# A cross-attention block on one core: the last two pairs of batches in another order, with the last probabilities turned through DRAM

## The chip, the cores and the metric

The kernel runs on one core of one Trainium2 chip. The metric is the device time of one execution in microseconds (us); lower is better. The kernel before and the changed kernel compute the same function in 32-bit floating point throughout.

## The reference

The inputs are x and a context, both [128 batches, 128 positions, 256], and the weights of one layer: four 256x256 projections, a 256x1024 W1, a 1024x256 W2, biases, and two sets of norm factors. There are 16 heads of 16. With mask = 0 position i attends only to positions below i, and row 0 of the probabilities is set to zero:

```python
q = (query @ Wq + bq).reshape(b, s, N_HEADS, D_K).transpose(0, 2, 1, 3)
k = (key @ Wk + bk).reshape(b, s, N_HEADS, D_K).transpose(0, 2, 1, 3)
v = (values @ Wv + bv).reshape(b, s, N_HEADS, D_K).transpose(0, 2, 1, 3)
scores = jnp.einsum('bhqd,bhkd->bhqk', q, k) / jnp.sqrt(jnp.float32(D_K))
allowed = j < i + mask
scores = jnp.where(allowed, scores, NEG_INF)
attn = jax.nn.softmax(scores, axis=-1)
if mask == 0:
    attn = attn.at[:, :, 0, :].set(0.0)
ctx = jnp.einsum('bhqk,bhkd->bhqd', attn, v).transpose(0, 2, 1, 3).reshape(b, s, d)
x = layer_norm(query + ctx @ Wo + bo, ln1_g, ln1_b)
ffn = jax.nn.relu(x @ W1 + b1) @ W2 + b2
out = layer_norm(x + ffn, ln2_g, ln2_b)
```

Key and values are both the context.

## The kernel before, in words

Two batches make a pair; there are 64 pairs, 0 to 63, and NP is 64. The work is a software pipeline over pairs: while one pair's scores are made, earlier pairs are in their feed-forward part. The order on each engine is written out by hand (a manual schedule): each engine executes its instructions in the order of the program, and waits by itself where an operand or a buffer isn't there yet. That holds for the DMAs too: SP (and ACT, where ACT issues them) waits in its own order, and what is queued behind a waiting DMA waits with it.

One pair p goes through these steps, each a function of the kernel:

- queries, keys and values: projections on TensorE (eight 256-wide matmuls each), copied out by ACT.
- `scores_both`: the scores of the lower and upper halves of the rows ("low" has 64 columns a head, "high" 128). `mask`, `mask_high`, `low_maximum` on VectorE; `exponential_by_head` on ACT, one instruction for each head (L840); `reciprocal` on VectorE and `sums` on GpSimd (L444), which multiplies 1024 columns by the reciprocal sums.
- `turn` (L463): VectorE transposes 32x32 blocks of the probabilities into the tile tb, in three thirds (two high, one low). `bring` (L478): sixteen DMAs move strip i, block j of tb to strip j, block i of the tile pT, SBUF to SBUF, 96 KB each. Together the two make the full transpose.
- `weigh` (L510, L520; the tile pc): probabilities times values. `context` copies to cxT. `attention_out` (po): the product with Wo, eight 256-wide matmuls. `attention_sum`, `both_stats`, `both_shifts`, `norm1`: residual and first norm, by VectorE, GpSimd and ACT; x1 is the result.
- `turn_x1`: VectorE transposes x1 into tbx; `across` sends it to DRAM in four DMAs (x1t, L246) and fetches it in one (x1T, L249).
- `combine_normed` (xS) and `Hidden`: the product with W1, in seven block products in place of eight; each is eight matmuls of 128 columns (L989). `run(1, 6)` runs products 1 and 6; `keep` (ACT, L999) copies product 1 out of its bank of PSUM, and `u2`, `u3`, `add2` to `add5` (VectorE) add the others up in hT. Product 3 accumulates on product 5's bank, after `add5` has read it. `again` takes bank 2 a second time, for product 5, once `keep` has emptied it. `relus` (L1020) follows on ACT.
- `combine_hidden` (hS, four GpSimd instructions) and `Second`: the product with W2, again in seven block products (L893; tiles pX, py, pz), added to the residual t2 by `add` (L928).
- `residual1` (GpSimd) makes the residual with its biases; `norm2` and `finish` (or `norm2_apart` and `finish_apart`, in a bank of PSUM with VectorE) the second norm; `store` (L684) writes the output.

PSUM has eight banks, and each product names the bank it takes. `step(p)` for p = 7 to 62 runs, in this order on TensorE: weigh(p-2), scores(p), the projections, attention_out(p-2), the W2 products of pair p-4, the W1 products of pair p-3. At its end SP issues, in order, the x1t sends and x1T fetch of pair p-2, the store of pair p-5 and the sixteen pT DMAs of pair p.

After the loop stands the ending, for p = 63, where no projections of a further pair are left. On TensorE: weigh(61), scores(63), attention_out(61), values(63), all seven W2 products of pair 59, weigh(62), six W1 products of pair 60, and so on to the W2 products of pair 62. Of pair 63's pT DMAs SP issues eight and ACT eight, after all three turns. The very last W2 product (pair 63) is done in two halves of 16 plain 256-wide matmuls (py_last, L1671); each half is added to t2 (L1675), gets its statistics (L1677, L1678), its epsilon on VectorE (L1679), its power of -0.5 on GpSimd (L1680), and two multiplications with the factors of the norm (L680, L681) before its store (L1684).

## Time and profile before

| what | value |
|---|---|
| median of 3 runs | 1505.72 us (1505.43 to 1507.54) |
| the profiled execution | 1507.01 us |
| its span in the trace | 1505.2 us |
| mean granted clock of TensorE | 0.994 |
| TensorE, ACT, GpSimd, VectorE busy | 98%, 88%, 87%, 85% |
| DMA, mean of the span | 136 GB/s |

The span is the time from the first to the last recorded instruction; the profiled execution takes 1.8 us more. Busy shares are means over the whole span, so they say little of the last 90 us, which this change is about. A row of the trace in order of time gives start, duration, engine, line of the code, operation, tiles (out<-in), how many instructions are merged in it, and in brackets the idle time ahead of it with what ended it. PE is TensorE, DVE VectorE, POOL GpSimd, SPq and ACTq the DMAs that SP and ACT issue.

### The profile page before, as it was taken

The numbers are of one execution on the slowest core, as the hardware profiler recorded it, in microseconds if no ns is written. First come the engines' busy times: TensorE is split into PE (matmuls) and PEld (weight loads), VectorE is DVE, ScalarE is ACT, GpSimd is POOL, SyncE is SP. The second block draws the span as 40 slices with busy tenths as digits, with TensorE's granted clock in tenths as the row PEclk, the third lists the DMA queues.
The fourth block names the chain that finished last, engine by engine and source line by source line (L and its number), as shares of the span: only waits on it lengthen the run. The fifth ranks groups of instructions, "written<-read, shape, count | busy, mean of one in ns | idle before, by whom it ended". The sixth has DMA issues, their size and how long they took to land.

```text
span 1505.2 us, 54159 instructions
## 1 busy us (share of the span) xinstructions
PE 1481.1 (98%) x19366; PEld 1383.7 (92%) x19366; DVE 1282.0 (85%) x2735; ACT 1319.3 (88%) x5277; POOL 1304.5 (87%) x1308
## 2 busy tenths in 40 slices
PE   8999999999999999999999999999999999999888
PEld 7788999999999999999999999999999999999887
DVE  7989888888888898898898888898898888888846
ACT  5667999999999999999999999999999999999843
POOL 6878888988988988988988988988988989889956
PEclk9999999999999999999999999999999999999989
DMA  8356656566656566656566666566666566664431
GB/s 198 85 116 140 151 141 132 141 144 134 157 132 142 138 144 136 153 139 140 134 145 141 151 141 138 137 141 142 149 141 141 134 143 141 150 139 114 124 78 50
DMA packets 415321, 204.66 MB, mean 136 GB/s; under 512 B 282448, under 2 KB 383056, under 8 KB 415056
## 3 DMA queue, kind: packets, MB, share of 16 engines
q1 hardware_dynamic: 412768, 199.34, 57.2%
q8 instruction: 159, 2.61, 0.8%
q10 hardware_dynamic: 2288, 1.85, 0.5%
q14 instruction: 106, 0.87, 0.2%
HBM read 70.26 MB, written 33.29 MB: 69 GB/s over the span
## 4 chain that ended last, share of the span: by engine, by line
PE 91%; DVE 3%; DMA 2%; ACT 1%; POOL 1%; SPq 1%; issue 1%; POOLq 0%; DVEq 0%; ACTq 0%
PE phs L989 25%; PE pX L893 10%; PE pq L268 8%; PE py L893 7%; PE pv L308 7%; PE pz L893 7%; PE po L539 7%; PE pk L268 7%; PE pss L391 6%; PE pc L520 4%; PE pc L510 2%; PE ph L777 1%; SPq L478 1%; DMA pT<-tb 1%; ACT sm L840 0%
## 5 line engine op out<-in xcount | busy, mean ns | idle before, releaser
L444 POOL TENSOR_TENSOR sm<-sm,rs 128x1024 f32<-128x1024 f32 x192 | 361.8, 1899 | 11.6 <-PE phs L989 7.8
L840 ACT ACTIVATE sm<-pss,nmx 128x128 f32<-128x128 f32 x944 | 328.5, 404 | 37.9 <-issue 33.6
L840 ACT ACTIVATE sm<-sm,nmx 128x64 f32<-128x64 f32 x944 | 313.8, 405 | 0.0
L463 DVE STREAM_TRANSPOSE tb<-sm 128x1024 f32<-128x1024 f32 x186 | 226.2, 1219 | 32.7 <-POOL sm L444 32.7
L840 ACT ACTIVATION_READ_ACCUMULATOR sm<-sm,nmx 128x1 f32 x912 | 235.4, 258 | 0.0
L1020 ACT ACTIVATE hT<-hT,b1e_c 128x256 f32<-128x256 f32 x480 | 204.4, 499 | 27.9 <-DVE hT L1011 27.9
L840 ACT ACTIVATION_READ_ACCUMULATOR sm<-pss,nmx 128x1 f32 x912 | 222.5, 244 | 0.0
L989 PE MATMUL phs<-xS,w1t 128*128 128x128 f32 x1440 | 172.2, 276 | 5.2 <-ACT hT L999 5.2
L989 PEld LDWEIGHTS phs<-xS,w1t 128*128 128x128 f32 x1440 | 167.0, 193 | 5.4 <-ACT hT L999 5.4
L862 POOL TENSOR_TENSOR hS<-hT 128x512 f32<-128x512 f32 x60 | 76.1, 1269 | 91.2 <-ACT hT L1020 90.2
L823 DVE TENSOR_REDUCE nmx<-pss 128x4 f32<-128x512 f32 x236 | 150.8, 680 | 0.0
L298 ACT ACTIVATE kT<-pk,bkh,half 128x256 f32<-128x256 f32 x252 | 130.6, 588 | 4.0 <-PE pk L268 4.0
L989 PE MATMUL phs<-x1T,w 128*128 128x128 f32 x960 | 127.4, 276 | 0.6 <-DMA x1T<-x1t 0.6
L893 PE MATMUL pX<-wt,hS 128*128 128x128 f32 x960 | 126.8, 275 | 0.0
L268 PE MATMUL pq<-xT,wq 128*128 128x256 f32 x504 | 125.4, 392 | 0.0
L539 PE MATMUL po<-wo,cxT 128*128 128x256 f32 x512 | 121.3, 380 | 0.8 <-ACT cxT L532 0.8
L308 PE MATMUL pv<-wv,cT 128*128 128x256 f32 x512 | 120.9, 379 | 0.0
L268 PE MATMUL pk<-cT,wk 128*128 128x256 f32 x504 | 119.2, 379 | 0.0
L989 PEld LDWEIGHTS phs<-x1T,w 128*128 128x128 f32 x960 | 117.5, 193 | 0.9 <-PE pX L893 0.7
L893 PEld LDWEIGHTS pX<-wt,hS 128*128 128x128 f32 x960 | 116.8, 192 | 0.0
L405 DVE TENSOR_TENSOR sm<-pss,neg 128x256 f32<-128x256 f32 (+1 forms) x276 | 108.2, 435 | 7.3 <-PE pss L363 2.5
L539 PEld LDWEIGHTS po<-wo,cxT 128*128 128x128 f32 x512 | 96.8, 190 | 14.6 <-ACT cxT L532 1.3
(167 smaller groups left out, 3915.9 us busy)
## 6 DMA issues: line engine op xcount, KB each, us to landing
pT<-tb SPq DMA_DIRECT2D x976, 96.0 KB, 2.2
x1t<-tbx SPq DMA_DIRECT2D x252, 64.0 KB, 3.0
x1T<-x1t SPq DMA_DIRECT2D x63, 256.0 KB, 3.0
out_dram<-t SPq DMA_DIRECT2D x63, 256.0 KB, 3.2
xb<-in_x_dram SPq DMA_DIRECT2D x124, 128.0 KB, 4.2
cb<-in_ctx_dram SPq DMA_DIRECT2D x124, 128.0 KB, 3.8
x<-in_x_dram SPq DMA_DIRECT2D x31, 512.0 KB, 4.6
w<-in_L_xattn_W_dram SPq DMA_DIRECT2D x2, 1024.0 KB, 7.7
```

What stands on the lines that cost most here:

```text
L268: nc.tensor.matmul(ps[:, m * TP : (m + 1) * TP], w[:, k, m * P : (m + 1) * P], src[:, k, :], start=(k == 0), stop=(k == KC - 1),)
L298: nc.scalar.activation(st["kT"][:, m, e, :], pk[:, m * TP : (m + 1) * TP], AF.Identity, bias=bkh[:, m, e : e + 1], scale=half[:, e : e + 1],)
L308: nc.tensor.matmul(pv[:, s * D : (s + 1) * D], st["cT"][:, k, s * P : (s + 1) * P], wv[:, k, :], start=(k == 0), stop=(k == KC - 1),)
L405: nc.vector.tensor_tensor(st["sm", hi][:, 4 * r : 4 * r + 4, :], st["sps", hi][r][:, : 4 * n].rearrange("p (n j) -> p n j", j=n), no[:, No ...
L444: nc.gpsimd.tensor_tensor(sm[:, part, :], sm[:, part, :], rs[:, :, None].to_broadcast([P, part.stop - part.start, n]), ALU.mult,)
L463: nc.vector.transpose(st["tb"][:, :, at : at + 256].rearrange("p j (n a) -> p n j a", a=32), st["sm", hi].rearrange("p h j -> p (h j)")[:, ...
L539: nc.tensor.matmul(po[:, s * D : (s + 1) * D], cxT[:, k, s, :], wo[:, k, :], start=(k == 0), stop=(k == KC - 1),)
L823: nc.vector.tensor_reduce(st["nmx", 1][:, 4 * r : 4 * r + 4], st["sps", 1][r].rearrange("p (n j) -> p n j", j=P), AX.X, ALU.max, negate=True,)
L840: nc.scalar.activation(sm[:, h, :], src, AF.Exp, bias=nmx[:, h : h + 1], scale=1.0, **({"accum_out": st["su", hi][:, h : h + 1]} if summed ...
L893: nc.tensor.matmul(out, left(k), right(k), start=(first and k == 0), stop=(k == K - 1), skip_group_check=True,)
L989: nc.tensor.matmul(ps[:, i * P : (i + 1) * P].rearrange("p (n a) -> p n a", a=32), left(i), right, start=(i == 0 and which not in self.ONT ...
L1020: nc.scalar.activation(self.hT[:, f], self.hT[:, f], AF.Relu, bias=b1e_c[:, f : f + 1], scale=1.0,)
```

## The change

Nothing is changed before step 62, and no product is added or removed. What is reordered or replaced:

- **Step 62**: four of the sixteen pT DMAs of pair 62 are issued before the fetch of x1T(60), twelve after it, and the store of pair 57 last.
- **`turn_x1` is split** into `send_x1` and `fetch_x1`, which the ending calls apart.
- **pair 63's probabilities**: `send` writes a third of tb (512 KB) to DRAM in one DMA as soon as that third is turned; `fetch` reads it back transposed in four DMAs of 128 KB. All are issued by SP; ACT issues none.
- **order of the ending**: pair 59's first W2 product comes before attention_out(61); six W1 products of pair 60 come before weigh(62), values(63) after it; the low exponentials are cut into 4, 4 and 8 with norm1(61) and keep in between; the W2 products of pairs 60 to 62 start before product 3 of the next pair's W1, and weigh(63) stands among those of pair 60. `Hidden` is given its own bank for product 5 in each pair, so that `again` isn't called there. Norms, residuals and stores are moved to fit, and pair 60's last two VectorE operations are called apart.
- **last tile**: the sum with t2, the statistics and the first multiplication stay in PSUM; epsilon is added by GpSimd; the first multiplication of the first half comes before `finish_apart(62)`.

The diff up to the ending:

```diff
                 )
         return pt
-    def across(dst, src, name, queue):
+    def out_across(src, name, queue):
         n = src.shape[2]
...
             queue.dma_start(
                 mid[i].rearrange("j b n -> b j n"), src[32 * i : 32 * i + 32]
             )
+        return mid
+    def back(dst, mid, queue):
         queue.dma_start(dst, mid.rearrange("i j b n -> (j b) i n"))
     def tokens(p, which):
...
                 "p (n j a) -> p n j a", j=NS, a=32
             ),
         )
+    def send(p, t):
+        st = states[p]
+        if "pT" not in st:
+            pT = st["pT whole"] = wide(f"pT_{p}").rearrange("p (i n) -> p i n", i=NS)
+            st["pT"] = pT.rearrange("p i (n a) -> p i n a", a=32)
+        at = slice(256 * t, 256 * t + 256)
+        mid = st["through", t] = dram.tile([NS, 32, NS, 256], F32, tag=f"pTt{t}", name=f"pTt{t}_{p}", bufs=1)
+        nc.sync.dma_start(mid.rearrange("i b j n -> (i b) j n"), st["tb"][:, :, at])
+    def fetch(p, t):
+        st = states[p]
+        mid = st.pop(("through", t))
+        for j in range(NS):
+            nc.sync.dma_start(
+                st["pT whole"][32 * j : 32 * j + 32, :, 256 * t : 256 * t + 256],
+                mid[:, :, j].rearrange("i b n -> b i n"),
+            )
     def bring(p, queue, which):
...
                 ps[:, s], t2[:, s], AF.Identity, bias=nb[:, s], scale=sd[:, s]
             )
-    def finish_apart(p):
+    def finish_apart(p, parts=(0, 1)):
         t2, ps = states[p]["t2"], states[p]["pb"]
-        nc.vector.tensor_tensor(ps, ps, g2_r[:, None, :].to_broadcast([P, 2, D]), ALU.mult)
-        nc.vector.tensor_tensor(t2, ps, be2_r[:, None, :].to_broadcast([P, 2, D]), ALU.add)
-        store(p)
-    def norm_alone(t2, mean, sd):
-        nc.vector.scalar_tensor_tensor(t2, t2, mean, g2_r, ALU.subtract, ALU.mult)
-        nc.vector.scalar_tensor_tensor(t2, t2, sd, be2_r, ALU.mult, ALU.add)
+        if 0 in parts:
+            nc.vector.tensor_tensor(ps, ps, g2_r[:, None, :].to_broadcast([P, 2, D]), ALU.mult)
+        if 1 in parts:
+            nc.vector.tensor_tensor(t2, ps, be2_r[:, None, :].to_broadcast([P, 2, D]), ALU.add)
+            store(p)
     def store(p):
         nc.sync.dma_start(
...
-    def turn_x1(p, queue=nc.sync):
+    def turn_x1(p):
+        send_x1(p)
+        fetch_x1(p)
+    def send_x1(p):
         st = states[p]
         tb = ffn.tile([P, NS, 4 * 32], F32, tag="tbx", name=f"tbx_{p}", bufs=1)
         nc.vector.transpose(
             tb.rearrange("p j (u a) -> p u j a", a=32),
             st["x1"].rearrange("p s (k j a) -> p (s k) j a", k=KC, a=32),
         )
+        st["mid"] = out_across(tb, f"x1t_{p}", nc.sync)
+    def fetch_x1(p):
+        st = states[p]
         x1T = ffn.tile([P, NS, 4 * 32], F32, tag="x1T", name=f"x1T_{p}")
-        across(x1T, tb, f"x1t_{p}", queue)
+        back(x1T, st.pop("mid"), nc.sync)
         st["x1T"] = x1T.rearrange("p i (s k a) -> p s i k a", s=2, k=KC)
     def turn_x1_on_pe(p):
...
         def __init__(self, p, banks=None):
             st = states[p]
-            self.WHERE = banks or self.WHERE
+            if banks:
+                self.WHERE, self.AGAIN = banks, {}
             self.p, self.x1T, self.xs = p, st["x1T"], st["xS"]
             self.hT = st["hT"] = ffn.tile([P, FC, TP], F32, tag="hT", name=f"hT_{p}", bufs=2)
             self.h = self.hT.rearrange("p (i e) (s t) -> p e s i t", e=2, s=2)
...
         norm2(p - 5)
         h.add4()
         h.relus((0, 2, 4, 6))
-        turn_x1(p - 2)
+        send_x1(p - 2)
+        if p < NP - 2:
+            fetch_x1(p - 2)
         h.add3()
         turn(p, 0, 0)
         states[p - 3]["rest"] = h
...
         residual1(p - 3)
         hidden_by_seven(p)
         finish(p - 5)
-        store(p - 5)
-        bring(p, nc.sync, LATE_FIRST)
+        if p < NP - 2:
+            store(p - 5)
+            bring(p, nc.sync, LATE_FIRST)
+        else:
+            bring(p, nc.sync, LATE_FIRST[:4])
+            fetch_x1(p - 2)
+            bring(p, nc.sync, LATE_FIRST[4:])
+            store(p - 5)
     third()
     fourth()
```

The calls of the ending (p = 63) after the change, in their order, several to a line; h and w are the current objects of `Hidden` (W1) and `Second` (W2):

```python
weigh(p - 2); context(p - 2); states[p - 4]["rest"].relus((1, 7, 3, 5)); scores_both(p); add_bo(p - 1)
combine_hidden(p - 4, POOL_ALONE); combine_normed(p - 3); mask(p, 0, B); mask(p, 0, A); mask_high(p, A)
exponential_by_head(p, 1, ONES, True); w = Second(p - 4, banks=(4, 7, 6)); w.run(1); attention_out(p - 2)
attention_sum(p - 2); w.run(2, 4, 5); w.add(0); mask_high(p, B); exponential_by_head(p, 1, TWOS, True)
w.add(1); joint = both_stats((p - 2,), ()); both_shifts(*joint); residual1(p - 3); w.run(6); w.add(2)
low_maximum(p); exponential_by_head(p, 0, ONES[:4], True); norm1(p - 2)
exponential_by_head(p, 0, ONES[4:], True); reciprocal(p, 1, ONE); reciprocal(p, 1, TWO); sums(p, 1, ONE)
sums(p, 1, TWO); w.run(3); w.add(4, 3); w.run(7); w.add(5); add_bo(p)
h = Hidden(p - 3, {1: 2, 2: 6, 6: 5, 7: 3, 5: 0, 4: 1}); h.run(1, 2, 6); h.keep()
exponential_by_head(p, 0, TWOS, True); send_x1(p - 2); h.u2(); h.run(7, 5); h.u3(); turn(p, 1, 0); send(p, 0)
fetch_x1(p - 2); reciprocal(p, 0, ALL); h.add5(); turn(p, 1, 1); send(p, 1); fetch(p, 0); h.run(4); h.add2()
weigh(p - 1); context(p - 1); values(p); h.run(3); h.add4(); h.relus((0, 2, 4, 6)); h.add3()
h.relus((1, 7, 3, 5)); sums(p, 0, ALL); turn(p, 0, 0); send(p, 2); fetch(p, 1); fetch(p, 2); values_out(p)
attention_out(p - 1); combine_normed(p - 2); attention_sum(p - 1); joint = both_stats((p - 1,), ())
both_shifts(*joint); later = both_stats((), (p - 5, p - 4))
h = Hidden(p - 2, {1: 2, 2: 6, 6: 5, 7: 3, 5: 0, 4: 7}); h.run(1, 2, 6); h.keep(); norm1(p - 1)
combine_hidden(p - 3, POOL_ALONE); residual1(p - 2); both_shifts(*later); h.u2(); h.run(7, 5); h.u3()
send_x1(p - 1); fetch_x1(p - 1); h.add5(); h.run(4); h.add2(); h.add4(); h.relus((0, 2, 4, 6))
w = Second(p - 3, banks=(1, 6, 4)); w.run(1, 2); h.run(3); h.add3(); w.run(4); w.add(0); w.run(6); w.add(2)
w.run(5); weigh(p); context(p); w.run(7); residual1(p - 1); combine_normed(p - 1); h.relus((1, 7, 3, 5))
norm2(p - 5); norm2(p - 4); attention_out(p); w.add(1); attention_sum(p); joint = both_stats((p,), ())
both_shifts(*joint); w.run(3); w.add(5, 3, 4); joint = both_stats((), (p - 3,)); both_shifts(*joint)
combine_hidden(p - 2, POOL_ALONE); h = Hidden(p - 1, {1: 2, 2: 0, 6: 3, 7: 7, 5: 5, 4: 6}); h.run(1, 2, 6)
h.keep(); norm1(p); h.u2(); h.run(7, 5); h.u3(); send_x1(p); fetch_x1(p); h.add5(); h.run(4); h.add2()
h.add4(); norm2_apart(p - 3, 4); h.relus((0, 2, 4, 6)); w = Second(p - 2, banks=(1, 2, 0)); w.run(1); h.run(3)
h.add3(); h.relus((1, 7, 3, 5)); w.run(2, 4, 5); w.add(0, 3, 1); w.run(6); w.add(2); finish(p - 5)
store(p - 5); finish_apart(p - 3, (0,)); w.run(3); w.add(4); finish_apart(p - 3, (1,)); w.run(7); w.add(5)
combine_normed(p); combine_hidden(p - 1, POOL_ALONE); joint = both_stats((), (p - 2,)); both_shifts(*joint)
residual1(p); finish(p - 4); store(p - 4); h = Hidden(p, {1: 4, 2: 3, 6: 7, 7: 5, 5: 6, 4: 1})
h.run(1, 2, 4, 6); h.keep(); h.u2(); h.run(7, 5); h.u3(); h.add5(); w = Second(p - 1, banks=(0, 7, 2))
w.run(1, 2); h.run(3); h.add2(); h.add4(); h.relus((0, 2, 4, 6)); h.add3(); h.relus((1, 7, 3, 5))
norm2_apart(p - 2, 3); w.run(4, 5); w.add(0, 3, 1); w.run(6); w.add(2); w.run(3); w.add(4); w.run(7); w.add(5)
joint = both_stats((), (p - 1,)); both_shifts(*joint); finish_apart(p - 2); norm2_apart(p - 1, 4)
```

The last tile:

```diff
     for s in range(2):
-        py = at_bank(1 + s, f"py_last_{s}")
+        py = at_bank(5 + s, f"py_last_{s}")[:, :D]
         for f in range(FC):
             nc.tensor.matmul(
-                py[:, :D], st["hT"][:, f, s * P : (s + 1) * P], w2[:, f, :],
+                py, st["hT"][:, f, s * P : (s + 1) * P], w2[:, f, :],
                 start=(f == 0), stop=(f == FC - 1),
             )
-        nc.vector.tensor_tensor(t2[:, s], py[:, :D], t2[:, s], ALU.add)
+        nc.vector.tensor_tensor(py, py, t2[:, s], ALU.add)
         bs = small.tile([P, 6], F32, tag="bs", name=f"bs_last_{s}", bufs=4)
-        nc.vector.bn_stats(bs, t2[:, s])
+        nc.vector.bn_stats(bs, py)
         nc.vector.bn_aggr(mv[:, s], bs)
-        nc.vector.tensor_scalar(sd[:, s], mv[:, s, 1:2], LN_EPS, None, ALU.add)
+        nc.gpsimd.tensor_tensor(sd[:, s], mv[:, s, 1:2], eps[:, 0], ALU.add)
         nc.gpsimd.tensor_tensor(sd[:, s], sd[:, s], power[:, 0], ALU.pow)
+        nc.vector.scalar_tensor_tensor(py, py, mv[:, s, 0:1], g2_r, ALU.subtract, ALU.mult)
         if s == 0:
             finish_apart(p - 1)
-        norm_alone(t2[:, s], mv[:, s, 0:1], sd[:, s])
+        nc.vector.scalar_tensor_tensor(t2[:, s], py, sd[:, s], be2_r, ALU.mult, ALU.add)
         nc.sync.dma_start(out[2 * NP - 2 + s], t2[:, s])
```

227 lines of the change are left out of this document (120 added, 107 removed).

## The prediction

> **What bounds the kernel now.** I read the page first, then the busy times by stretch, then TensorE's rows in order of time, its waits, and the queues of the engines it had waited for. TensorE is the bound, and only the last pair of batches leaves it idle.
>
> ```profile
> PE 1481.1 (98%) x19366; PEld 1383.7 (92%) x19366; DVE 1282.0 (85%) x2735; ACT 1319.3 (88%) x5277; POOL 1304.5 (87%) x1308
> ...
> 1420.00:1440.00 20.00, 15.13 (x194) 14.71 (x194) 10.23 (x30) 12.25 (x61) 11.82 (x15) 0.83 0.47 120
> 1440.00:1460.00 20.00, 14.82 (x184) 14.21 (x184) 10.54 (x19) 10.62 (x24) 15.20 (x20) 0.83 0.43 102
> 1460.00:1480.00 20.00, 19.44 (x165) 18.93 (x164) 9.65 (x25) 4.88 (x11) 14.25 (x17) 1.00 0.21 58
> ```
>
> In each stretch the second number is TensorE's busy time, and the third from the end the clock granted to it. From 1420 to 1460 it loses 10 us to idling, and some more to a clock of 0.83. Its rows show where (in brackets the idle time ahead of a row, and its releaser):
>
> ```profile
> 1407.06 2.84 PE L989 MATMUL phs<-xS,w1t 128*128 128x128 f32 x24
> 1409.74 1.06 PE L989 MATMUL phs<-x1T,w 128*128 128x128 f32 x8
> ...
> 1412.52 0.43 PE L510 MATMUL pc<-pT,vd 128*32 128x64 f32 x16
> ...
> 1413.99 1.62 PE L391 MATMUL pss<-kT,qT 32*64 32x128 f32 x64
> ...
> 1430.45 0.66 PE L510 MATMUL pc<-pT,vd 128*32 128x64 f32 x16 [4.87 <-DMA x1t<-tbx]
> ...
> 1439.05 1.06 PE L989 MATMUL phs<-x1T,w1t 128*128 128x128 f32 x8
> ...
> 1451.63 2.07 PE L989 MATMUL phs<-xS,w1t 128*128 128x128 f32 x8 [5.18 <-ACT hT L999]
> ...
> 1456.77 0.43 PE L510 MATMUL pc<-pT,vd 128*32 128x64 f32 x16
> ...
> 1479.79 2.02 PE L989 MATMUL phs<-x1T,w 128*128 128x128 f32 x16 [0.56 <-DMA x1T<-x1t]
> ...
> 1492.58 7.07 PE L1671 MATMUL py_last<-w,hT 128*128 128x256 f32 x32
> ```
>
> Prices first. One product of eight matmuls (one of seven in W1 or W2) takes (1409.74-1407.06)/3 = 0.89 us; the weighing of a pair (pc) takes 1413.99-1412.52 = 1.47; eight 256-wide matmuls are a quarter of the last row, 1.77. Idle time is 4.87+5.18+0.56 = 10.61. After each of the two long stalls the matmuls run slowly: from 1430.45 to 1439.05 stand a pc and five products, 5.94 at full speed, in 8.60: 2.66 lost. From 1451.63 to 1456.77 stand three products, 2.68, in 5.14: 2.46 lost. After the 0.56 nothing of that size is lost. So the ending holds 10.61+5.12 = 15.7 us, and no reordering can win more from TensorE.
>
> The queues tell what it waited for:
>
> ```profile
> 1413.07 1.79 SPq L246 DMA_DIRECT2D x1t<-tbx  x4
> 1417.58 0.38 SPq L249 DMA_DIRECT2D x1T<-x1t  x1
> ...
> 1418.61 10.06 SPq L478 DMA_DIRECT2D pT<-tb  x16
> ...
> 1444.79 5.72 SPq L478 DMA_DIRECT2D pT<-tb  x8
> 1444.79 6.10 ACTq L478 DMA_DIRECT2D pT<-tb  x8
> 1450.99 0.59 ACT L999 COPY hT<-phs 128x512 f32<-128x512 f32 x1 [6.47 <-DMA pT<-tb]
> 1451.47 1.09 ACT L613 ACTIVATE t<-t,nb,sd 128x256 f32<-128x256 f32 x2
> ```
>
> The first stall: pair 62's sixteen pT DMAs leave SP only by 1428.67, and weigh(62) comes on TensorE right after pair 59's W2 products. The second: ACT issues eight of pair 63's pT DMAs, and the copy of the hidden layer of pair 61 (keep), without which bank 2 isn't free for product 5, stands behind them.
>
> **The change part by part.** *SP in step 62.* Four of the sixteen pT DMAs go into the gap between 1414.86 (end of the x1t row) and 1417.58; the store goes behind all. At 10.06/16 = 0.63 each the other twelve end at 1417.96+7.55 = 1425.5, 3.2 earlier, so weigh(62) could start at 1430.45-3.2 = 1427.3. x1T(60) is fetched when it was, at 1417.58. *Order on TensorE.* Scores end at 1415.61. Ahead of weigh(62) now stand seven W2 products, attention_out(61) and six W1 products of pair 60: 13 x 0.89+1.77 = 13.4, so TensorE gets there at 1429.0, 1.7 behind the data. Cover: six products, whose x1T(60) lands by 1417.58+3.0 (row below). If they were late, up to 4.87 is back. The first stall goes, 4.87+2.66.
>
> *keep without DMAs ahead of it, product 5 in its own bank 0.* Nothing on ACT waits for a DMA queue now: 5.18+2.46 go, unless weigh(63), the next thing late, takes their place. That is the heart of the sum: sixteen direct DMAs become three sends of 512 KB to DRAM and three times four fetches, all on SP.
>
> ```profile
> pT<-tb SPq DMA_DIRECT2D x976, 96.0 KB, 2.2
> x1t<-tbx SPq DMA_DIRECT2D x252, 64.0 KB, 3.0
> x1T<-x1t SPq DMA_DIRECT2D x63, 256.0 KB, 3.0
> out_dram<-t SPq DMA_DIRECT2D x63, 256.0 KB, 3.2
> ...
> x<-in_x_dram SPq DMA_DIRECT2D x31, 512.0 KB, 4.6
> ...
> L99 SPq DMA_DIRECT2D x<-in_x_dram x33: 376/803/1762, 0.8 to 1383.6; - x33
> ...
> L246 SPq DMA_DIRECT2D x1t<-tbx x252: 303/433/2042, 70.0 to 1474.9; - x126
> ...
> L478 SPq DMA_DIRECT2D pT<-tb x976: 507/591/2162, 63.8 to 1449.9; - x196
> ...
> 1423.37 0.44 ACT L840 ACTIVATE sm<-sm,nmx 128x64 f32<-128x64 f32 x1
> ...
> 1425.69 0.40 ACT L840 ACTIVATE sm<-sm,nmx 128x64 f32<-128x64 f32 x1
> ...
> 1428.54 3.75 POOL L444 TENSOR_TENSOR sm<-sm,rs 128x1024 f32<-128x1024 f32 x2
> ...
> 1441.79 1.24 DVE L463 STREAM_TRANSPOSE tb<-sm 128x1024 f32<-128x1024 f32 x1
> ```
>
> The first rows give the us from issue to landing, the next three the ns of issuing (least, median, most). A send is the x load turned round, and twice a store: between 3.2 and 6.4, I take 4.6 as nearest in size. A fetch of 128 KB lies between the rows of 3.0 and 4.6; 3.6. Issuing costs 0.43 (32 partitions in four runs, as x1t) to 0.59 (as pT): 0.5.
>
> When is the last third ready? The low exponentials, first and last of eight being 2.32 apart (0.33 each), start near 1423.4: 16 x 0.33 = 5.3, with norm1(61) (1.09) and keep (0.59) between, end near 1430.5. GpSimd does what it did up to the end of the high sums, 1432.3, in another order; a low sum of 1.88 gives 1434.2, and the transpose of 1.24, behind two adds on VectorE, 1435.6. SP sets the rest, since it waits in order. The first high sum now precedes add_bo and ends near 1429.2, its transpose near 1430.4: send 0 from 1430.5 lands at 1435.1; four fetches 1437.1; send 2, queued behind them, lands at 1441.7; the last of its fetches is issued at 1443.2 and lands at **1446.8**. TensorE needs it after 26 products, three sets of 1.77 and pc(62) from 1415.61: 23.2+5.3+1.5, that is **1445.6**. So 1.2 us of idling is added. Ends: nothing, with landings of 4.0 and 3.0; 4.5, with issues of 0.80 as the x row's median and landings of 5.0 and 4.0.
>
> Does 1.2 us slow the clock? The 0.56 did not, the 4.87 did; nearer is 0.56, so 0, with 2.5 as the other end. The Trainium skill ("TensorE: Matmul & The Clock Gate", section "Why this matters for your kernels") sets the limit near 3 us of idling. By that rule 1.2 is free and 4.5 is not, and the trace agrees at 0.56 and 4.87.
>
> Against the change speaks the Trainium skill's "DMA: Bandwidth & Descriptors", section "Anatomy of one DMA": some 2.0 us of each DMA are fixed, mostly the receipt of the write, heaviest for HBM, so a way through DRAM pays it twice in a row. By its 2.0 plus bytes over 436 GB/s a hop of 512 KB is an estimated 3.2 us, and the sum would be 1.2 better than mine; the row of 4.6 disagrees.
>
> *x1 apart, W1 and W2 interleaved.*
>
> ```profile
> 1412.45 1.71 ACT L1020 ACTIVATE hT<-hT,b1e_c 128x256 f32<-128x256 f32 x4 [0.42 <-DVE hT L1011]
> ...
> 1412.96 0.65 DVE L1014 TENSOR_TENSOR hT<-hT,phs 128x512 f32<-128x512 f32 x1
> ```
>
> x1(62)'s sends stand behind SP's wait for send 2 now, and leave by 1443.7+4 x 0.43 = 1445.4; landed 2.6 after the last one's issue, fetched 3.0: 1450.6. TensorE wants it at 1446.8+1.47+0.89+1.77+0.89 = 1451.8: hidden, with 1.2 to spare, and a later fetch of pair 63 moves both alike. Product 3, which waits for add5 to free its bank, has a W2 product ahead of it. x1(63) is sent right after u3(62). From there to its first W1 product TensorE has ten products, 8.9 us; u3 and the transposition (0.65 each by the second row, 512 columns as well), the sends (1.72), their landing (2.57) and the fetch (3.0) make 8.6. So the 0.56 goes too, if only by 0.3. Norms and stores move to engines and queues that idle there: 0; if GpSimd, with one more set of shifts, were late, the cover is four W2 products, 3.6.
>
> *Last tile.*
>
> ```profile
> 1494.16 0.20 POOL L585 TENSOR_TENSOR sd<-mv,eps 128x2 f32<-128x2 f32 x1 [2.83 <-DVE mv L580]
> ...
> 1501.19 0.72 POOL L1680 TENSOR_TENSOR sd_last<-sd_last,power 128x1 f32<-128x1 f32 x1 [2.96 <-DVE sd_last L1679]
> ...
> 1499.83 0.42 DVE L1675 TENSOR_TENSOR t<-py_last,t 128x256 f32<-128x256 f32 x1
> ...
> 1500.95 0.15 DVE L1679 TENSOR_SCALAR sd_last<-mv_last 128x1 f32<-128x1 f32 x1
> ...
> 1501.95 0.48 DVE L681 SCALAR_TENSOR_TENSOR t<-t,sd_last,be_r 128x256 f32<-128x256 f32 x1 [0.45 <-POOL sd_last L1680]
> ```
>
> VectorE's 0.15 (0.24 to the start of the power) becomes a GpSimd add of 0.20 with a handover: +0.05. The first multiplication was done beside the power already, as the 0.45 of waiting shows. The first half's chain loses the 0.15, and the second half's add, which began 0.18 after TensorE's end (1499.65), may start that much sooner: -0.15. Statistics taken from PSUM aren't in the trace; the add that reads it took 0.42. Together 0, plus or minus 0.2.
>
> **Sum.** 15.7-1.2 = 14.5 off the span of 1505.2: 1490.7. The profiled execution took 1507.0, 1.8 more than its span and 1.3 more than the median of 1505.7; the forecast for the median is 1505.7-14.5 = 1491.2.
>
> **Rivals.** *The way through DRAM is slower (B):* a stall of 4.5 and the clock's 2.5 at weigh(63): 1505.7-15.7+7.0 = 1497.0. For it: x-sized issues at 0.80, three transfers of 512 KB in flight near 1437. Against it: in that stretch SP carries little else.
>
> *The change does not do what it says (C):* the transposes of pair 63 might wait for the earlier send to land, where waits are set for whole tiles. The second would wait for send 0 (1435.1) and end at 1436.3, its send land at 1440.9, the third end at 1442.1 and hold attention_sum(62), which frees bank 5, until 1442.7. TensorE wants that bank after 16 products, three sets of 1.77 and pc(62), at 1436.6: 6.1 plus 2.5, 1498.6. Against it stand the two rows of hT: VectorE writes some strips at 1412.96 while ACT is at others, which interleave with them, from 1412.45 to 1414.16.
>
> *SP becomes the bound (D), slower than before:* with the x row's most, 1.76 an issue, send 0 lands at 1430.5+1.76+4.2 = 1436.4, thirteen more issues end at 1459.3, the last lands at 1462.5: 16.9 of idling and 2.5 of clock, 1509.4. It decides from 1.5 us an issue. Against it: the median of every row of issues is under half of that when transfers are small.
>
> **How the numbers follow.** Forecast 0.72, B 0.17, C 0.05, D 0.04, something between C and D that ends level 0.02. The forecast's own range is 1488.5 (no stall, the tail 0.2 better, runs up to 1 us apart) to 1494. With B inside, the range is 1488.5 to 1498. A measurement of this kernel can tell about 0.2%, 3 us: faster 0.94, same 0.02, slower 0.04.
>
> **What would show it.** Right: one idle time of TensorE over 0.3 us, ahead of pc of pair 63, 0 to 2.5; a clock of 1.00 in every stretch from 1420 on; no pT DMA on ACT; TensorE's last matmul near 1485; the tail 5.5 us as before. Wrong: an idle time ahead of pc of pair 62 (SP), ahead of product 6 of pair 61 with VectorE as releaser (C), or of more than 3 at pc of pair 63 with a clock under 1 behind it (B, D).

## The result and the profile after

The changed kernel took 1492.01 us (median of 4 runs, 1491.65 to 1494.95), the kernel before, in 4 runs, 1506.34 (1505.43 to 1507.54): a ratio of 0.9909, interval 0.9892 to 0.9926, so it is faster, clear of the scatter of the runs. The forecast was 1491.2, range 1488.5 to 1498.0. The span went from 1505.2 to 1489.9 us.

To compare the two traces from the same point on, take the *ending*: the time from the start of weigh(61) on TensorE to the end of its last matmul. Before, that is 1492.58 + 7.07 - 1412.52 = 87.13 us. The rows below make it 1477.44 + 7.07 - 1412.06 = 72.45. So the ending gave 14.68 of the 15.3 us of span; 0.46 lies ahead of weigh(61), where the two kernels do the same, and 0.16 behind the last matmul. That first part differs from run to run by more than many of the effects here (weigh(61) starts at 1411.61 in a4 below and at 1415.42 in a3), which is why the ending is compared and not the span.

The busy times by stretch (second number TensorE, third from the end its clock):

```profile
1420.00:1440.00 20.00, 19.21 (x237) 18.19 (x237) 16.88 (x40) 16.77 (x69) 17.34 (x24) 1.00 0.75 212
1440.00:1460.00 20.00, 19.82 (x252) 19.24 (x251) 11.94 (x28) 9.88 (x22) 18.09 (x27) 1.00 0.39 90
1460.00:1480.00 20.00, 19.87 (x167) 19.42 (x166) 11.83 (x31) 7.17 (x17) 18.04 (x22) 1.00 0.17 53
```

TensorE is busy 19.2 to 19.9 us in each stretch of 20, where it was 15.1, 14.8 and 19.4, and the clock is 1.00 where it was 0.83. What idle time is left, TensorE's rows show:

```profile
1412.06 0.43 PE L532 MATMUL pc<-pT,vd 128*32 128x64 f32 x16
...
1428.74 0.43 PE L532 MATMUL pc<-pT,vd 128*32 128x64 f32 x16
...
1435.63 2.05 PE L1017 MATMUL phs<-x1T,w 128*128 128x128 f32 x16 [0.79 <-DMA x1T<-x1t]
...
1445.00 1.13 PE L920 MATMUL pX<-wt,hS 128*128 128x128 f32 x8 [0.17 <-DVE t L955]
...
1446.95 0.43 PE L532 MATMUL pc<-pT,vd 128*32 128x64 f32 x16
...
1463.67 1.06 PE L920 MATMUL pX<-wt,hS 128*128 128x128 f32 x8
1464.87 2.02 PE L1017 MATMUL phs<-x1T,w 128*128 128x128 f32 x16
...
1477.44 7.07 PE L1719 MATMUL py_last<-w,hT 128*128 128x256 f32 x32
```

Neither weigh(62) (1428.74) nor weigh(63) (1446.95) has a bracket: both weighings find their data there. What is left is 0.79 ahead of pair 61's first W1 product, 0.17 ahead of product 6 of pair 60, and 0.13 without a bracket just ahead of 1464.87 (from 1464 to 1466 TensorE is busy 1.87 of 2 us). That is 1.09, where the forecast had 1.2: the same size, at another place. SP's rows say a part of why the 0.79 is there:

```profile
1414.56 3.02 SPq L500 DMA_DIRECT2D pT<-tb  x4
1417.76 0.46 SPq L252 DMA_DIRECT2D x1T<-x1t  x1
1418.26 8.37 SPq L500 DMA_DIRECT2D pT<-tb  x12
1426.74 0.51 SPq L703 DMA_DIRECT2D out_dram<-t  x1
1427.36 1.90 SPq L246 DMA_DIRECT2D x1t<-tbx  x4
1430.46 0.62 SPq L481 DMA_DIRECT2D pTt<-tb  x1
1431.62 0.86 SPq L252 DMA_DIRECT2D x1T<-x1t  x1
1432.59 0.59 SPq L481 DMA_DIRECT2D pTt<-tb  x1
1434.36 1.76 SPq L487 DMA_DIRECT2D pT<-pTt  x4
1436.17 0.52 SPq L481 DMA_DIRECT2D pTt<-tb  x1
1436.97 5.27 SPq L487 DMA_DIRECT2D pT<-pTt  x8
```

x1 of pair 61 is sent (1427.36) behind pair 62's last twelve pT DMAs and a store, and its fetch (1431.62) stands behind send 0. In the chain of work that ended last it takes 3.96 us from its issue:

```profile
1431.62 3.96 DMA x1T<-x1t
```

It lands at 1435.58, and TensorE, free since 1434.84, starts at 1435.63. The other part is the transfer itself: in a1 below, where no send of probabilities is in flight, the same fetch takes 2.8 us. With 2.8 from the same issue it would have landed at 1434.4, ahead of TensorE. So the sends cost x1T(61) twice, in SP's order and in the time to landing. The way through DRAM itself, issues in ns (least, median, most) and medians in us to landing:

```profile
pTt<-tb SPq DMA_DIRECT2D x3, 512.0 KB, 4.3
pT<-pTt SPq DMA_DIRECT2D x12, 128.0 KB, 3.5
```

```profile
L487 SPq DMA_DIRECT2D pT<-pTt x12: 303/432/837, 1434.4 to 1441.8; - x12
L481 SPq DMA_DIRECT2D pTt<-tb x3: 519/591/617, 1430.5 to 1436.2; - x3
```

Forecast were 4.6 and 3.6 with issues of 0.5. The last fetch was issued at 1441.8; with 3.5 to land its data is there at 1445.3, and TensorE comes at 1446.95: about 1.6 us to spare.

### The profile page after: what moved, and what is told of

Read it like the earlier page. It is cut to its first block, busy times and chain, and to the rows that moved or that the text cites. A ratio compares the mean times of both kernels' runs of the same rounds, so it can differ in the third digit from the quotient of the medians.

```text
span 1489.9 us, 54159 instructions
## 1 busy us (share of the span) xinstructions
PE 1476.3 (99%) x19366; PEld 1378.6 (93%) x19366; DVE 1281.8 (86%) x2733; ACT 1318.3 (88%) x5277; POOL 1305.4 (88%) x1314
## 4 chain that ended last, share of the span: by engine, by line
PE 94%; DVE 1%; ACT 1%; POOL 1%; DMA 1%; issue 0%; ACTq 0%; SPq 0%; POOLq 0%; DVEq 0%
PE phs L1017 25%; PE pX L920 11%; PE pq L271 8%; PE py L920 7%; PE pz L920 7%; PE pv L311 7%; PE po L561 7%; PE pk L271 7%; PE pss L394 6%; PE pc L542 4%; PE pc L532 2%; PE ph L804 1%; ACT sm L867 0%; PE py L824 0%; PE py_last L1719 0%
## 5 line engine op out<-in xcount | busy, mean ns | idle before, releaser
L466 DVE STREAM_TRANSPOSE tb<-sm 128x1024 f32<-128x1024 f32 x186 | 226.2, 1219 | 31.9 <-POOL sm L447 30.6
```

What stands on the lines that cost most here:

```text
L466: nc.vector.transpose(st["tb"][:, :, at : at + 256].rearrange("p j (n a) -> p n j a", a=32), st["sm", hi].rearrange("p h j -> p (h j)")[:, ...
```

## The experiments

**The theory**, as the prediction has it: the 15.7 us of the ending before are idle time that follows from the order on SP and ACT, plus what the slow clock adds behind each stall; the change removes both because TensorE has other products at hand and no engine's work stands behind a DMA. The rivals were: product 5's wait was for its bank and not for ACT's queue; the way through DRAM is what helps; the clock's loss is no cost of its own, since the next wait ends when it ends anyway. Twelve kernels: six change the kernel before (e), six the kernel after (a). "Ending" is measured as above, from the same two rows of each trace.

| kernel | median, us | ratio to before (interval) | ending, us |
|---|---|---|---|
| before | 1506.34 | 1 | 87.13 |
| after | 1492.01 | 0.9909 (0.9892 to 0.9926) | 72.45 |
| e1: before + step 62's new order on SP | 1503.04 | 0.9985 (0.9975 to 0.9995) | 84.23 |
| e2: before + own bank for product 5 | 1506.69 | 1.0009 (0.9999 to 1.0020) | 87.48 |
| e3: before, all pT DMAs on SP | 1508.13 | 1.0021 (1.0006 to 1.0036) | 87.26 |
| e4: before + the way through DRAM | 1505.94 | 1.0002 (0.9989 to 1.0016) | 85.69 |
| e5: before + matmuls over the whole stalls | 1508.05 | 1.0012 (1.0002 to 1.0021) | 88.33 |
| e6: before + half of these | 1505.08 | 1.0001 (0.9990 to 1.0013) | 86.07 |
| a1: after, pT direct, all on SP | 1494.37 | 0.9925 (0.9904 to 0.9945) | 75.47 |
| a2: after, step 62's old order on SP | 1493.99 | 0.9921 (0.9904 to 0.9938) | 74.02 |
| a6: after, both of these | 1496.79 | 0.9946 (0.9923 to 0.9969) | 77.94 |
| a3: after, old last tile | 1492.58 | 0.9920 (0.9905 to 0.9934) | 72.40 |
| a4: after, store(57) later | 1491.59 | 0.9906 (0.9890 to 0.9923) | 72.67 |
| a5: after, each send in four | 1494.51 | 0.9927 (0.9912 to 0.9943) | 75.52 |

Each ratio is against runs of before on the same chip. The intervals of after and of the a kernels overlap, so what tells those apart are the rows of their traces. An ending is that of one execution, and it holds one thing that an edit doesn't set: a stall of the same length is followed by one or by two slow stretches of the clock, or by none, each worth up to 1.7 us (the last section shows by what). Where that decides, the text says so.

### e1: step 62's order on SP alone

```diff
-        turn_x1(p - 2)
+        send_x1(p - 2)
+        if p < NP - 2:
+            fetch_x1(p - 2)
...
-        store(p - 5)
-        bring(p, nc.sync, LATE_FIRST)
+        if p < NP - 2:
+            store(p - 5)
+            bring(p, nc.sync, LATE_FIRST)
+        else:
+            bring(p, nc.sync, LATE_FIRST[:4])
+            fetch_x1(p - 2)
+            bring(p, nc.sync, LATE_FIRST[4:])
+            store(p - 5)
```

> The kernel before with the changed order on SP in step 62 alone (four pT DMAs ahead of the fetch of x1T(60), twelve behind it, the store last). Theory (the prediction's terms): pair 62's pT lands 3.2 us earlier, at 1427.3 on the clock of before, where TensorE arrives at 1425.6; the wait ahead of weigh(62) shrinks from 4.87 to about 1.7, and the slow clock behind it (2.66) goes wholly or in part: span 1499.3 to 1502.0, against 1505.2. Rival (the six W1 products put ahead of weigh(62) are what cures the first stall, SP's order is worth nothing by itself): span above 1504.

TensorE's row of weigh(62):

```profile
1428.08 0.43 PE L513 MATMUL pc<-pT,vd 128*32 128x64 f32 x16 [3.19 <-DVE tbx L748]
```

The wait fell from 4.87 to 3.19. Counted from weigh(61), the ending is 2.90 shorter: 1.7 of wait, and one slow stretch of the clock behind it in place of two (1.7 lost in place of 2.66). The medians of ten and more runs say 0.15%, 2.3 us. So the reorder on SP is worth 2 to 3 us by itself. The rest of the first stall, 3.19 and 1.7, needs TensorE to have something else to do. The bracket names tbx, and in before x1t; but weigh reads pT, whose last DMA was issued at 1428.08 in before and took 2.2 to land: 1430.3, just ahead of 1430.45.

### e2: own bank for product 5

```diff
-            self.WHERE = banks or self.WHERE
+            if banks:
+                self.WHERE, self.AGAIN = banks, {}
...
-    h = Hidden(p - 2)
+    h = Hidden(p - 2, {1: 2, 6: 5, 2: 6, 7: 3, 4: 7, 5: 0})
```

> The kernel before with a bank of its own (0) for product 5 of pair 61 alone; ACT still issues eight of pair 63's pT DMAs ahead of keep. Theory (ACT is blocked by the DMAs, and product 3 needs add5, which needs keep): products 5 and 4 run early, the idle time moves to product 3; gain 0 to 1.5, span 1503.7 to 1505.2. Rival (the bank is the cause of the second stall): 5.18 and 2.46 go, span 1497.6.

The first row is TensorE's, the second ACT's queue:

```profile
1454.28 2.05 PE L990 MATMUL phs<-xS,w 128*128 128x128 f32 x8 [6.05 <-DVE hT L1009]
```

```profile
1444.78 6.36 ACTq L478 DMA_DIRECT2D pT<-tb  x8
```

Product 5 no longer waits, but product 3 does, for 6.05 us: the sums it needs are built on the copy that keep makes, and keep still starts only when ACT's eight issues are over (1451.14). The ending is 0.35 longer, where 0 to 1.5 shorter was expected; the rival asked for 7.6 shorter. The bank was where the wait showed, not its cause; that rival falls. A wait put down to a buffer can have the same root as the data behind it.

### e3: all sixteen pT DMAs of pair 63 on SP

```diff
-    bring(p, nc.scalar, EVERY[:8])
+    bring(p, nc.sync, EVERY[:8])
```

> The kernel before with all sixteen pT DMAs of pair 63 issued by SP, none by ACT, and nothing else changed. Theory (the next thing late is weigh(63)): SP issues from 1444.8 at 0.63 each to 1454.9, the last lands near 1456.7, TensorE would be there at 1449.2; the second stall moves to weigh(63) and grows to 7.5, with 2.5 of slow clock behind it: span 1505 to 1508. Rival (ACT's queue is the whole cause of the second stall): span 1497.6.

```profile
1455.39 0.65 PE L510 MATMUL pc<-pT,vd 128*32 128x64 f32 x16 [7.46 <-DMA pT<-tb]
```

```profile
1443.37 10.05 SPq L478 DMA_DIRECT2D pT<-tb  x16
```

ACT is free, and the stall is at weigh(63) instead, 7.46 where 7.5 was expected: sixteen issues in one queue take 10.05 us. The ending is as long as in before, though the second stall, with its clock, is 1.1 longer (7.46 + 1.2 against 5.18 + 2.46): the first stall, which this edit doesn't touch, had one slow stretch behind it in place of two. Taking the DMAs off ACT gains nothing as long as TensorE has no other work at that time.

### e4: the way through DRAM in the old order

The calls; `send` and `fetch` are those of the change.

```diff
     turn(p, 1, 0)
+    send(p, 0)
     h.add5()
     turn(p, 1, 1)
+    send(p, 1)
+    fetch(p, 0)
     attention_sum(p - 1)
     turn(p, 0, 0)
-    bring(p, nc.sync, EVERY[8:])
-    bring(p, nc.scalar, EVERY[:8])
+    send(p, 2)
+    fetch(p, 1)
+    fetch(p, 2)
```

> The kernel before with pair 63's probabilities sent through DRAM as in the change (three sends, twelve fetches, all on SP, each third sent when it is turned), the order on the other engines as before. Theory (the trip pays only in the new order): ACT is free, but the last fetch lands near 1454.2 and TensorE waits for it from 1449.2, 5.0 at weigh(63), with 2.5 of slow clock: span 1504 to 1506. Rival (the trip through DRAM is the heart of the gain): the second stall and its clock go, span 1497.6 or less.

```profile
1453.85 0.66 PE L529 MATMUL pc<-pT,vd 128*32 128x64 f32 x16 [6.38 <-DMA pT<-pTt]
```

No difference in the medians: weigh(63) waits 6.38, more than the 5.0 expected. The ending is 1.44 shorter, but not by the trip: the first stall, which this edit doesn't touch (4.71 here), had one slow stretch behind it in place of two, 1.3 us less, while the second stall with its clock is as long as in before (6.38 + 1.3 against 5.18 + 2.46). The trip hides nothing by itself; the rival that it is what helps falls.

### e5 and e6: matmuls in the stalls

Products of the identity go to a free bank just ahead of weigh(62) and of product 5. They compute nothing that is used; what they do is keep TensorE from idling.

```diff
+    filler = at_bank(1, "filler_0")
+    for _ in range(34):
+        nc.tensor.matmul(filler[:, :P], ident, ident, start=True, stop=True)
     weigh(p - 1)
...
-    h.run(7, 5)
+    h.run(7)
+    filler = at_bank(1, "filler_1")
+    for _ in range(38):
+        nc.tensor.matmul(filler[:, :P], ident, ident, start=True, stop=True)
+    h.run(5)
```

That is e5; e6 has 17 and 19 in place of 34 and 38.

> The kernel before with 34 and 38 more matmuls of 128x128 on the identity, into a bank that nothing reads, laid into the two long stalls (ahead of weigh(62), and between products 7 and 5 of pair 61); the result is as before. It fills about 3.8 and 4.2 us of waits of 4.87 and 5.18 and changes nothing else. Theory (the slow matmuls behind a stall are a loss of their own, 2.66 and 2.46): the granted clock stays at 1.00 and the span falls by about 5.1 to 1499.5 to 1501. Rival (what follows a stall is bound by the other engines anyway, so a faster clock only lengthens the next wait): span 1503 to 1505.2.

```profile
1426.74 7.76 PE L1523 MATMUL filler<-ident 128*128 128x128 f32 x68
...
1447.72 8.65 PE L1575 MATMUL filler<-ident 128*128 128x128 f32 x76
```

The sizes were wrong: each call on 32-bit operands is two instructions in the trace (x68 for 34 calls), so the fillers took 7.69 and 8.48 us to the next matmul, twice what was meant and longer than the stalls. With these lengths the theory gives 7.69 + 8.48 - 4.87 - 5.18 - 2.66 - 2.46 = +1.0; measured is +1.20, with a clock of 0.999 to 1.00 in every stretch. That the 5.12 of the clock is real time, and goes when TensorE doesn't idle, agrees with this. e6 has the lengths that were meant.

> The filled stalls again with half the filler: each 32-bit matmul of the program is two instructions of 0.11 us in the trace, so the earlier kernel's filler took 7.69 and 8.48 us where 4.87 and 5.18 were idle. Now 34 and 38 instructions, 3.8 and 4.2 us; the result is as before. Theory (the slow matmuls behind a stall are a loss of their own, 2.66 and 2.46; it also says 7.69+8.48-4.87-5.18-2.66-2.46 = 1.0 longer for the earlier kernel, which took 1.2): from weigh(61) to the end of the last matmul 82 us in place of 87.13, span 1499.5 to 1501.5, clock 1.00. Rival (the other engines bind behind a stall): 86 or more, span 1503 or more.

TensorE's rows behind two of the waits, then SP's and ACT's queues:

```profile
1430.68 0.43 PE L510 MATMUL pc<-pT,vd 128*32 128x64 f32 x16 [2.25 <-DMA x1t<-tbx]
...
1450.46 1.16 PE L989 MATMUL phs<-xS,w1t 128*128 128x128 f32 x8 [2.09 <-ACT hT L999]
```

```profile
1417.33 11.47 SPq L478 DMA_DIRECT2D pT<-tb  x16
```

```profile
1442.47 7.25 ACTq L478 DMA_DIRECT2D pT<-tb  x8
```

A miss: 86.07, where 82 was expected and the rival had 86 or more. The clock did stay at 1.00 in every window of 2 us from 1424 to 1460, so the 5.12 is gone, and it came back elsewhere. The sixteen issues took 11.47 in place of 10.06, and ACT's eight 7.25 in place of 6.10: 2.56 in all, ahead of both waits, which are still waits. For x1T(63) 1.23 is waited in place of 0.56, and 0.34 is new, for VectorE. 82.0 + 2.56 + 0.67 + 0.34 = 85.6; the last 0.5 has no row. So the number is the rival's, and so is a part of the reason: product 5 starts 1450.46 - 1411.56 = 38.90 us after weigh(61), against 39.11 in before. In the old order a TensorE that isn't slowed reaches the next wait sooner, and the queues decide when that ends. Part of the 2.56 is one SP issue of 2.0 us in this execution (last section); but the ten runs, 1503.69 to 1508.53, show no gain of that size either. The clock's loss is a gain only where nothing late stands behind it.

### a1: pair 63's probabilities brought direct

```diff
-    send(p, 0)
     fetch_x1(p - 2)
...
-    send(p, 1)
-    fetch(p, 0)
...
-    send(p, 2)
-    fetch(p, 1)
-    fetch(p, 2)
+    bring(p, nc.sync, EVERY)
```

> The changed kernel with sixteen direct pT DMAs, all on SP after the third turn, in place of the sends and fetches of pair 63. Theory (the order is worth most of it, the trip through DRAM about 1 us): SP issues from 1435.4 to 1445.5, the last lands near 1447.5, TensorE waits 0.5 to 2 ahead of weigh(63), and less ahead of pair 61's first W1 product: span 1490 to 1491.7, against 1489.9. Rival (the trip is the heart): span 1495 or more.

TensorE's row of weigh(63), SP's row, and the busy times behind the wait:

```profile
1448.37 0.32 PE L532 MATMUL pc<-pT,vd 128*32 128x64 f32 x8 [2.30 <-DMA pT<-tb]
```

```profile
1435.42 11.11 SPq L500 DMA_DIRECT2D pT<-tb  x16
```

```profile
1450.00:1452.00 2.00, 2.00 (x33) 1.83 (x24) 0.00 (x0) 1.22 (x3) 0.62 (x1) 0.50 0.34 84
```

Without the way through DRAM weigh(63) waits 2.30, and the clock halves behind it until 1452.1, some 1.7 us; the wait of 0.79 for x1T(61) is gone: its fetch leaves 18.84 us after weigh(61) in place of 19.56, with no send ahead of it, and takes 2.8 in place of 3.96, with none in flight. The ending is 3.02 longer, not the 1 expected, because 2.30 of idling was enough for the clock. Without that the trip is worth about 1.3; whether the clock's 1.7 comes on top is decided by where the stall falls (last section).

### a2 and a6: step 62's old order, alone and with a1

```diff
-            bring(p, nc.sync, LATE_FIRST[:4])
-            fetch_x1(p - 2)
-            bring(p, nc.sync, LATE_FIRST[4:])
-            store(p - 5)
+            fetch_x1(p - 2)
+            store(p - 5)
+            bring(p, nc.sync, LATE_FIRST)
```

> The changed kernel with SP's old order at the end of step 62 (fetch of x1T(60), store, sixteen pT DMAs). Theory (the six products ahead of weigh(62) cover most of it): a wait of about 1.3 ahead of weigh(62), and the sends of x1(61) about 1 us later, which mostly falls together with it: span 1490.5 to 1492. Rival (SP's order cures the first stall): 4.9 and the clock's 2.7 come back, span 1497.5.

```profile
1431.04 0.43 PE L532 MATMUL pc<-pT,vd 128*32 128x64 f32 x16 [1.98 <-DMA x1t<-tbx]
```

weigh(62) waits 1.98, the later x1T(61) 0.32, and the clock stays at 1.00: 1.57 more. a6 is a2 and a1 together: what is left of the change is the order on the compute engines, the banks and the last tile.

> The changed kernel with both of SP's edits taken back: the old order at the end of step 62, and sixteen direct pT DMAs of pair 63 on SP in place of the way through DRAM. What is left is the order on the other engines with the banks. Theory (the order is worth most; each of the two adds 1.5 to 3): waits of about 2 ahead of weigh(62) and 2 ahead of weigh(63), one of them with 1.7 of slow clock; from weigh(61) to the last matmul 75.5 to 77.5 us (87.13 before, 72.45 changed), span 1493 to 1495.5. Rival (the order pays only with both of SP's edits): 80 or more, span 1498 or more.

TensorE's rows, then the busy times behind the first wait:

```profile
1431.15 0.43 PE L532 MATMUL pc<-pT,vd 128*32 128x64 f32 x16 [2.33 <-DMA x1t<-tbx]
...
1450.95 0.32 PE L532 MATMUL pc<-pT,vd 128*32 128x64 f32 x8 [0.69 <-issue]
...
1457.47 2.05 PE L1017 MATMUL phs<-x1T,w 128*128 128x128 f32 x16 [1.37 <-DMA x1T<-x1t]
```

```profile
1432.00:1434.00 2.00, 2.00 (x54) 1.65 (x43) 1.28 (x3) 0.91 (x3) 1.74 (x1) 0.56 0.18 39
```

87.13 - 77.94 = 9.19 of the 14.68 come with the order, the banks and the last tile; 5.49 need the two edits on SP (a1 and a2, one at a time, cost 3.02 and 1.57), 1.7 of it the clock's. In before, by themselves, the reorder gave 2.90 and the trip nothing of its own (e1, e4). The ending is 0.4 over what was expected: one slow stretch came, as forecast, but the waits are 2.33, 0.69 and 1.37, 4.4 together, where about 4 was forecast, and the last of them, for x1T(62), whose sends stand behind the sixteen pT DMAs on SP, was not in the forecast at all. The six runs lie from 1494.2 to 1502.46, so the two shares are those of these traces and not exact.

### a3: the old last tile

```diff
-        nc.vector.tensor_tensor(py, py, t2[:, s], ALU.add)
+        nc.vector.tensor_tensor(t2[:, s], py, t2[:, s], ALU.add)
...
-        nc.vector.bn_stats(bs, py)
+        nc.vector.bn_stats(bs, t2[:, s])
...
-        nc.gpsimd.tensor_tensor(sd[:, s], mv[:, s, 1:2], eps[:, 0], ALU.add)
+        nc.vector.tensor_scalar(sd[:, s], mv[:, s, 1:2], LN_EPS, None, ALU.add)
...
-        nc.vector.scalar_tensor_tensor(py, py, mv[:, s, 0:1], g2_r, ALU.subtract, ALU.mult)
...
-        nc.vector.scalar_tensor_tensor(t2[:, s], py, sd[:, s], be2_r, ALU.mult, ALU.add)
+        norm_alone(t2[:, s], mv[:, s, 0:1], sd[:, s])
```

> The changed kernel with the last tile as before (sum and statistics in SBUF, epsilon on VectorE, the first multiplication after it), in the changed kernel's banks. Theory (the last tile's edit is worth 0 plus or minus 0.2): from the end of the last matmul to the end of the span 5.4 to 5.6 us, against 5.39; span 1489.7 to 1490.2. Rival (the sum in PSUM and the epsilon on GpSimd shorten the tail): 0.5 or more longer.

From the last matmul's end to the span's end it takes 5.58 us, against 5.55 in before and 5.39 in after: 0.2 for the last tile's edit, which no median here can show. The span, 1493.4, is over the forecast because weigh(61) starts 3.4 us later in this execution; the ending itself is 72.40. In after, the rows of the second half on VectorE and GpSimd:

```profile
1485.02 0.43 DVE L1725 BATCH_NORM_STATS2 bs_last<-py_last 128x6 f32<-128x256 f32 x1
```

```profile
1485.75 0.19 POOL L1727 TENSOR_TENSOR sd_last<-mv_last,eps 128x1 f32<-128x1 f32 x1 [2.57 <-DVE mv_last L1726]
1486.02 0.55 POOL L1728 TENSOR_TENSOR sd_last<-sd_last,power 128x1 f32<-128x1 f32 x1
```

The statistics from PSUM take 0.43, the epsilon 0.19 and the power 0.55 where before's second half took 0.72: all within what the forecast had.

### a4: store(57) behind the second send

```diff
             bring(p, nc.sync, LATE_FIRST[4:])
-            store(p - 5)
...
     send(p, 1)
+    store(p - 6)
     fetch(p, 0)
```

> The changed kernel with the store of pair 57 moved from the end of step 62 to behind the second send of pair 63, so that x1(61) is sent at once. Theory (the wait of 0.79 ahead of pair 61's first W1 product is SP's: the store stands ahead of x1(61)'s sends): the sends leave about 0.7 earlier, the wait falls to 0.1 to 0.3, span 1489.2 to 1489.5. Rival (x1T(61) is slowed by the first send, which is in flight beside it): wait and span unchanged.

```profile
1428.95 0.43 PE L532 MATMUL pc<-pT,vd 128*32 128x64 f32 x16 [0.59 <-DMA x1t<-tbx]
...
1435.39 2.05 PE L1017 MATMUL phs<-x1T,w 128*128 128x128 f32 x16 [0.35 <-DMA x1T<-x1t]
```

The wait for x1T(61) fell from 0.79 to 0.35, but not because the data came sooner. Counted from weigh(61), x1(61)'s sends left at 15.36 (15.30 in after), the fetch took 3.82 (3.96), and the product that needs it started at 23.78 (23.57). TensorE came later instead, after a new wait of 0.59 at weigh(62). The ending, 72.67, is no shorter than after's, and the two medians are 0.4 apart, within either's runs. No gain is shown, and since the sends didn't leave earlier, the run decides nothing between the store and the rival; that the transfer is slow beside a send, 3.8 to 4.2 in after, a2, a3 and a4 against 2.8 in a1 (and 2.9 in a5, beside smaller sends), speaks for the rival. Why weigh(62), whose transfers stand ahead of the store in both kernels, waits here and not in after lies in SP's row: its twelve issues took 8.46 against 8.37, and its first four 3.63 against 3.02, which also ate what the store's move was to win. That is no effect of the edit that could be shown.

### a5: each send in four DMAs of 32 partitions

```diff
-        nc.sync.dma_start(mid.rearrange("i b j n -> (i b) j n"), st["tb"][:, :, at])
+        for i in range(NS):
+            nc.sync.dma_start(mid[i], st["tb"][32 * i : 32 * i + 32, :, at])
```

> The changed kernel with each send cut into four DMAs of 32 partitions, so that SP issues twelve sends in place of three: nine more issues of 0.43, 3.9 us. Theory (SP's order of issuing sets when pT lands, and there is about 1 us of slack): the first W1 product of pair 61 waits about 1.9 in place of 0.79, weigh(63) about 1; the clock stays at 1.00; span 1491 to 1493. Rival (SP has room and the transfers themselves set the time): span within 0.3 of 1489.9.

TensorE's row of pair 61's first W1 product, and the busy times behind it:

```profile
1438.79 2.60 PE L1018 MATMUL phs<-x1T,w 128*128 128x128 f32 x16 [2.01 <-DMA x1T<-x1t]
```

```profile
1440.00:1442.00 2.00, 2.00 (x12) 2.00 (x11) 0.68 (x6) 0.70 (x2) 1.69 (x6) 0.53 0.84 233
```

Four issues take 2.71 us where one took 0.62, and x1T(61), behind them in SP's order, lands later: 2.01 of waiting. The wait was forecast (1.9). Wrong in the forecast were the clock's part, again some 1.7, and a wait of 1 at weigh(63), which has none. Of the span, 1494.9 where 1491 to 1493 was expected, 1.9 lies ahead of weigh(61); the ending is 3.07 longer than after's. The clock halves from 1440.1 to 1443.5, when TensorE has been at work again for 1.3 us.

## Why the prediction was right

**The first stall.** It put 4.87 + 2.66 down as gone, with six W1 products as cover. Measured: no wait at weigh(62), which starts at 1428.74 (forecast 1429.0). Of the 1.7 that TensorE was to come behind the data, 1.1 was used up: SP's last pT issue ended at 1426.63 and not at 1425.5. The term is right, but it belongs to two edits together: e1 has the one alone (2.90), a2 the other (1.57 lost without SP's).

**The second stall.** It said that keep, behind ACT's DMAs, is the cause and the bank a by-product. e2 shows this, and so does e3, where ACT issues no pT DMA and keep starts at 1443.00 in place of 1450.99. It also said that the next thing late would be weigh(63), and e3 and e4 show just that (7.46, 6.38) where TensorE's order is the old one.

**The way through DRAM: the step that failed.** The sum has "1.2 us of idling is added" at weigh(63), data at 1446.8 and TensorE at 1445.6. Measured: data at 1445.3, TensorE at 1446.95, no wait. Send 0 was issued at 1430.46 (forecast 1430.5), and its fetches began at 1434.36 (1435.1); send 2 went at 1436.17 (1437.1); the last fetch took 3.5 (3.6). Each term was a little long, most of all the landing of a send, 4.3 for 4.6, and they add up to 1.5. TensorE took 1446.95 - 1415.09 = 31.9 from the end of the scores, where the next product starts, in place of 30.0: 0.79 + 0.17 of idling that the forecast didn't have, and 0.9 spread over thirty groups of matmuls beyond their rounded prices. The sum went by the row of 4.6 and not by the estimated 3.2, and the row was the better price. The fit behind the 3.2 is stated by the Trainium skill ("DMA: Bandwidth & Descriptors", section "Anatomy of one DMA") for DMAs that GpSimd issues; these are issued by SP and took 4.3. Had the landings been as forecast, weigh(63) would still not have waited (1446.8 against 1446.95): the 1.2 was mis-sized on both sides.

**The wait that was left out.** "One idle time over 0.3, ahead of pc of pair 63" was wrong in its place: it is ahead of pair 61's first W1 product. The prediction reckoned x1T of pairs 60, 62 and 63, and not of 61, whose fetch stands behind a send that it had moved there itself and runs beside it. That 0.79 took the place of the 1.2 is luck: one term too many and one too few, of about the same size. What the sum has right is the 15.7: the ending lost 14.68 and holds 1.09 of new idling, 15.77 together.

**The clock.** It took 0 for a wait of about 1, and the clock was 1.00. Its reason, that 1.2 is nearer to 0.56 than to 4.87, was a guess; it holds, since in no trace was the clock slowed by a window with less than 1.96 us of idling (last section). The loss was not far, though: a1, a5 and a6 halved the clock after 2.30, 2.01 and 2.33 us. The Trainium skill's limit near 3 us ("TensorE: Matmul & The Clock Gate", section "Why this matters for your kernels"), which the prediction weighed, is too high by these three rows.

**x1 of pair 63, and the last tile.** The 0.56 went, as reckoned; 0.13 is left there, and no DMA is named as its end. The tail moved by 0.16, within 0 plus or minus 0.2; bn_stats on PSUM took 0.43.

**The rivals.** B needed landings of 5.0 and issues of 0.80: they were 4.3 and 0.43 to 0.59. C: the second send left at 1432.59, before send 0 had landed and its fetch begun (1434.36), so the second turn had not waited for it. D needed 1.5 us an issue; the longest of the fifteen took 0.84.

## What to carry to other kernels

An issue queue is a resource like an engine: before blaming the buffer that a wait is put down to, look at what stands ahead of the releaser in its engine's own order, DMA issues included. A stall goes when the waiting engine has other work and the data comes sooner; here the two halves gave 9.2 and 5.5 us of the 14.7 together, and no part put alone into the old order gave more than 2.9. When work is moved into a queue, reckon every item behind the place, also the one that wasn't late before: x1T(61) was missed in that way.
